# A four-layer pre-norm transformer stack: narrow attention's probabilities and the first attention's queries and keys turned in 64-row halves, ALiBi distances kept once, a value bias carried through the output weights

## The chip, the cores and the metric

The kernel runs on one core of a Trainium2 chip, in fp32 throughout. The metric is the device time of one execution in microseconds; the time given is the median of several runs, and a profile of one execution stands beside it.

## The reference

The input x has 16 sequences of 256 rows of 128 numbers. Four pairs of attention and feed-forward follow, each on the layer norm of x and added to x:

```python
x = x + L0_attn(norm(x))   # 16 heads of 64; queries and keys l2-normalised, scaled; 2 null keys; ALiBi; causal
x = x + L0_ffn(norm(x))    # 128 -> 512 -> gelu -> 128
x = x + L1_attn(norm(x))   # latent of 64; 16 heads of 8, one key and value head for all; causal
x = x + L1_ffn(norm(x))    # gated, then 512 -> 512 -> 512, then 128
x = x + L2_attn(norm(x))   # 16 heads of 64, biases on q, k and v; no mask
x = x + L2_ffn(norm(x))    # 8 experts, the best one for each row
x = x + L3_attn(norm(x))   # 16 heads of 8; window of 128
x = x + L3_ffn(norm(x))    # a gate with the row before
```

In the first attention the score of head h is `8 * (q . k) + dist * slope[h]`, where `dist` is minus the distance of query and key and `slope[h]` falls with h from 0.71 to 1/256. In the third, the value is `xn @ Wv + bv`, and the output `attention @ value @ Wo + bo`.

## The kernel before

The work of each sequence (a batch, b) is cut into steps: `step(engine, rank, ns, emit, r, w, m)` names an engine, a rank (what should come first), an estimate of its length and the tiles that it reads, writes or changes. Nothing is emitted at once. `plan.run()` walks a model of the engines and emits step after step: on each engine the lowest rank among those that could start soon, at most 12 ranks ahead of the first TensorE step that is still open. For TensorE a step also has a `mode`, the shape in which the array is used: "T" for all 128 rows and columns, "S" for two tiles of 64 rows, "O" for two of 64 columns, "S4" and "O4" for four tiles of 32 rows or columns. The plan adds 130 ns where the mode changes. Tiles come from homes with a fixed number of places: eight PSUM banks "t" of 512 columns, three "Q" and three "K", six "pT", six "probs", eight "r", and so on. A step that asks for a place waits until one is free. Each engine carries out its queue strictly in the order that comes out, and waits by semaphores. `evac` copies a PSUM bank into SBUF on ACT or DVE, whichever the plan takes.

Layers are ranked one after the other: 16 batches of the first attention at 16 ranks each, then of the second at 12, and so on; the steps of a batch's preparation lie one batch ahead. Feed-forward steps of two batches follow their attention.

First attention. `prep0` norms and turns x, projects it to queries, keys (`project(n, c)`: n is twice the row block i plus 1 for keys, c the half of the heads) and values. For each raw tile ACT squares, DVE sums over the heads' 64 columns, POOL takes the root (`rsqrt`), DVE multiplies (`scaled`), and TensorE turns four 128x128 blocks into a bank, which goes to Q by `evac`, or to K with the scale of queries and keys (`kqs`) on ACT. Sixteen tables `bias`, one for each head, are made by DVE from the distances `dist`; `first0` adds one to the scores and takes the row minimum of the negated sum. `wide_unit` works on four heads: scores, exponential (`second0`), division on POOL, turned probabilities, products, then `wide_out` through the output weights. It turns its probabilities in two 64-row halves already (line 491):

```python
for z in range(2):
    r, c = slice(64 * z, 64 * z + 64), j * (w // 2) + i * 64
    nc.tensor.transpose(t[z].t[:, c:c + 64], probs[pair].t[r, j, a:a + P], ident[r, r])
```

The halves use the two row tiles of the array at the same time and write into two banks.

Second and last attention. `narrow_unit` has three units to a batch. Four banks of scores (S4), mask and minimum on DVE (line 563), exponentials on ACT, then four turns of four 128x128 blocks each (line 581, mode T), a copy of each bank to "pT", and 16 products of 128 columns in four 32-column tiles (O4). The row sums come out of the products through a column of ones.

Third attention. `prep2` makes queries, keys and values; DVE adds a row `bv`, spread over the partitions by a load, to every values tile (line 1063). `bias_x` adds the output's bias `a2bo` to x on POOL.

Weights. The first load of weights fills `wA`; `to_w1` brings the second layer's into the place that the ALiBi tables held, after the first attention, and `to_w2` the third's into `wA`. These run on SP, as do all large loads.

Lines in the profile: 367 is every product (`mm`), 383 and 385 copies on ACT and DVE, 371 the root on POOL, 431 a turned norm, 474 the division on POOL, 491 and 581 turned probabilities, 744 a small DVE step on the sums, 756 turned queries and keys, 1063 the values' bias.

Of the kernel before, what the change touches and what calls it, by code (L numbers as in the profile page):

```python
# [25 lines left out]
    ("a2bq", 8), ("a2bk", 8),  # L26
# [205 lines left out]
def preln_d4_kernel(ctx: ExitStack, tc: tile.TileContext, x_in, vecs, rows, bv2, nullk, nullv,  # L232
# [50 lines left out]
    bv = cp.tile([P, 1024], F32, tag="bv", name="bv")  # L283
    nc.sync.dma_start(out=bv, in_=bv2.broadcast_to([P, 1024]))
# [74 lines left out]
    plan.home("r", many(sp, "r", 8, [512]))  # L359
# [6 lines left out]
    def mm(o, lhsT, rhs, start=True, stop=True, **kw):  # L366
        nc.tensor.matmul(o, lhsT, rhs, start=start, stop=stop, **kw)  # L367

# [72 lines left out]
    def bias_x(p, name, b):  # L441
        step("POOL", p, 670, lambda e: nc.gpsimd.tensor_tensor(x_of(b), x_of(b), row_over(name, 2), ALU.add), m=[X[b]])  # L442


    def wide_unit(q, b, u, st, widths, starts, blocks, first, second, kept=None):
# [36 lines left out]
        for pair in range(2):  # L482
# [3 lines left out]
            def turn(e, pair=pair, t=t):  # L486
                for j in range(2):
                    for i, a in enumerate(starts):
                        for z in range(2):
                            r, c = slice(64 * z, 64 * z + 64), j * (w // 2) + i * 64  # L490
                            nc.tensor.transpose(t[z].t[:, c:c + 64], probs[pair].t[r, j, a:a + P], ident[r, r])
# [52 lines left out]
    def narrow_unit(q, b, u, st, mask, mkey):  # L544
# [30 lines left out]
        for k in range(4):  # L575
            t, h = get("t"), get("pT")
            pT.append(h)

            def turn(e, k=k, t=t):
                for g in range(4):  # L580
                    nc.tensor.transpose(t.t[:, g * P:(g + 1) * P], probs[g // 2].t[:, g % 2, k * P:(k + 1) * P], ident)  # L581

            step("PE", q + 8 + k, 436, turn, r=probs, w=[t], mode="T")
            evac(q + 8 + k, h, t, lambda h=h, t=t: (h.t, t.t))
# [4 lines left out]
        def products(e):  # L589
# [3 lines left out]
            for k in range(4):  # L593
                hh, kc = (k, 0) if u == 0 else (2 * u - 2 + k // 2, k % 2)
                a = (256 if hh == 3 else 0) + qc * P
                for g in range(4):
                    mm(o.t[32 * g:32 * g + 32, a:a + P], st["v"](kc, g, hh), pT[k].t[:, g * P:(g + 1) * P],
                       u == 0 and k == 0, u == 2 and k == 3, skip_group_check=True)

        step("PE", q + 11.9, 900, products, r=[st["V"]] + pT, m=[o], mode="O4")  # L600
# [50 lines left out]
    bias_pool = top.enter_context(tc.tile_pool(name="a0c", bufs=1))  # L651
# [8 lines left out]
    A0, A1 = 0, first[1, 0]  # L660
    wqkv = wA[:, w0_at["qkv"]:w0_at["qkv"] + 3072]
# [825 lines left out]
```

## Time and profile before

| | us |
|---|---|
| median of 3 runs | 2208.14 |
| lowest and highest | 2207.95, 2212.46 |
| profiled execution, its own time | 2214.85 |
| its span, first to last instruction | 2213.1 |

The mean granted TensorE clock of the profiled execution is 0.990 of full speed. Its DMA engines move 57.78 MB, most of it in the first 60 us and around the loads of weights. The first TensorE instruction starts at 19.45 us, when its weights have landed. The stretches by layer: the first attention to about 640 us, the second with its feed-forward to about 1172, the third to about 1840, where the experts begin to overlap with the last attention (from 1849), and a last stretch of that attention alone from about 2040.

How to read it: a line of the timeline has start, length, engine, line, operation, output and inputs, then rows*columns of the array tile and the shape. A product is two records, since each fp32 product is made in two passes; a turn is one. Lengths of TensorE records overlap[...], so rates are read from starts.

### The profile page before, as it was taken

How to read it: one execution, taken by the hardware profiler on the slowest of the kernel's cores; microseconds unless marked ns; L12 is line 12 of the kernel's file. 1: busy time of each engine (PE TensorE's matmuls, PEld its weight loads, DVE VectorE, ACT ScalarE, POOL GpSimd, SP SyncE). 2: the span in 40 equal slices, each digit the busy share in tenths (PEclk: the TensorE clock that was granted, in tenths of full speed). 3: DMA queues.
4: the chain of work that ended last, by engine and by line, in shares of the span. 5: the costliest groups of instructions: out<-in, count | busy, mean ns of one | idle time of the engine just before them, and what ended most of it. 6: DMA issues, size and time to landing. Idle time of an engine off the chain costs nothing.

```text
span 2213.1 us, 57690 instructions
## 1 busy us (share of the span) xinstructions
PE 2141.7 (97%) x20879; PEld 1576.0 (71%) x20879; DVE 1657.2 (75%) x6401; ACT 1669.9 (75%) x4735; POOL 1054.0 (48%) x1987
## 2 busy tenths in 40 slices
PE   6999999999999999999999999999999999998997
PEld 3767777777776566665666678888888787786775
DVE  5898888889788575666655557877766788787995
ACT  5988888989889776677756567776666577777995
POOL 6997787878851111111103235554543855226331
PEclk9999999999999999999999999999999999999998
DMA  7000000000020000000000000000432000451000
GB/s 173 2 2 2 2 2 2 2 2 2 2 92 2 1 2 1 1 1 1 1 1 1 1 1 7 7 6 3 120 111 82 26 5 19 133 164 28 12 12 11
DMA packets 58590, 57.78 MB, mean 26 GB/s; under 512 B 27824, under 2 KB 48832, under 8 KB 58304
## 3 DMA queue, kind: packets, MB, share of 16 engines
q1 hardware_dynamic: 55504, 49.06, 7.9%
q0 software_dynamic: 2048, 4.20, 0.6%
q8 instruction: 165, 2.70, 0.5%
q14 instruction: 121, 0.99, 0.1%
q10 hardware_dynamic: 752, 0.83, 0.1%
HBM read 43.85 MB, written 10.22 MB: 24 GB/s over the span
## 4 chain that ended last, share of the span: by engine, by line
PE 78%; DVE 10%; POOL 6%; ACT 3%; issue 2%; DMA 1%; another core or an unknown queue 0%; SPq 0%; POOLq 0%; ACTq 0%; DVEq 0%
PE t5x L367 9%; PE t4x L367 8%; PE t7x L367 8%; PE t2x L367 8%; PE t3x L367 7%; PE t0x L367 7%; PE t1x L367 7%; PE t6x L367 7%; PE t0x L581 1%; PE t1x L581 1%; PE t2x L581 1%; PE t3x L581 1%; PE t5x L581 1%; PE t4x L581 1%; PE t6x L581 1%
## 5 line engine op out<-in xcount | busy, mean ns | idle before, releaser
L442 POOL TENSOR_TENSOR x<-x,row_sb 128x256 f32<-128x256 f32 x48 | 35.0, 728 | 31.9 <-DVE xn1x L411 16.0
L404 POOL TENSOR_SCALAR ln_rs1x<-ln_mv1x 128x2 f32<-128x2 f32 x24 | 4.6, 193 | 76.3 <-DVE ln_mv1x L400 73.4
L991 POOL TENSOR_TENSOR x<-x,sq1x 128x512 f32<-128x512 f32 x4 | 5.1, 1280 | 73.2 <-DVE sq1x L989 73.2
L474 POOL TENSOR_SCALAR probs4x<-probs4x,sums6x 128x256 f32<-128x256 f32 (+2 forms) x40 | 17.6, 457 | 38.5 <-DVE sums6x L469 16.9
L474 POOL TENSOR_SCALAR probs2x<-probs2x,sums6x 128x256 f32<-128x256 f32 (+2 forms) x40 | 17.6, 458 | 37.4 <-DVE sums6x L469 21.5
L474 POOL TENSOR_SCALAR probs2x<-probs2x,sums2x 128x256 f32<-128x256 f32 (+2 forms) x44 | 22.2, 519 | 25.8 <-DVE sums2x L469 25.5
L404 POOL TENSOR_SCALAR ln_rs0x<-ln_mv0x 128x2 f32<-128x2 f32 x21 | 4.0, 193 | 63.2 <-DVE ln_mv0x L400 60.2
L371 POOL TENSOR_TENSOR ss0x<-ss0x,mhalf 128x16 f32<-128x16 f32 x11 | 31.9, 2902 | 2.7 <-DVE ss0x L744 2.6
L371 POOL TENSOR_TENSOR ss2x<-ss2x,mhalf 128x16 f32<-128x16 f32 x11 | 32.3, 2934 | 1.6 <-DVE ss2x L744 1.3
L404 POOL TENSOR_SCALAR ln_rs3x<-ln_mv3x 128x2 f32<-128x2 f32 x22 | 4.2, 193 | 58.2 <-DVE ln_mv3x L400 53.2
L371 POOL TENSOR_TENSOR ss1x<-ss1x,mhalf 128x16 f32<-128x16 f32 x11 | 31.9, 2898 | 0.2 <-DVE sums3x L469 0.2
L371 POOL TENSOR_TENSOR ss3x<-ss3x,mhalf 128x16 f32<-128x16 f32 x11 | 31.9, 2896 | 0.0
L474 POOL TENSOR_SCALAR probs4x<-probs4x,sums4x 128x256 f32<-128x256 f32 (+2 forms) x44 | 21.3, 499 | 21.8 <-DVE sums4x L469 21.4
L371 POOL TENSOR_TENSOR ss4x<-ss4x,mhalf 128x16 f32<-128x16 f32 x10 | 29.4, 2942 | 4.7 <-DVE ss4x L744 2.9
L404 POOL TENSOR_SCALAR ln_rs4x<-ln_mv4x 128x2 f32<-128x2 f32 x23 | 4.4, 193 | 57.1 <-DVE ln_mv4x L400 53.8
L474 POOL TENSOR_SCALAR probs4x<-probs4x,sums2x 128x256 f32<-128x256 f32 (+2 forms) x44 | 23.2, 541 | 17.1 <-DVE sums2x L469 9.3
L474 POOL TENSOR_SCALAR probs2x<-probs2x,sums0x 128x256 f32<-128x256 f32 (+2 forms) x44 | 19.4, 459 | 23.8 <-DVE sums0x L469 21.9
L371 POOL TENSOR_TENSOR ss5x<-ss5x,mhalf 128x16 f32<-128x16 f32 x10 | 29.0, 2898 | 0.0
L474 POOL TENSOR_SCALAR probs2x<-probs2x,sums4x 128x256 f32<-128x256 f32 (+2 forms) x44 | 22.1, 515 | 14.1 <-DVE sums4x L469 10.0
L991 POOL TENSOR_TENSOR x<-x,sq0x 128x512 f32<-128x512 f32 x4 | 5.1, 1280 | 45.2 <-DVE sq0x L989 45.2
L474 POOL TENSOR_SCALAR probs5x<-probs5x,sums3x 128x256 f32<-128x256 f32 (+2 forms) x44 | 20.9, 487 | 12.1 <-DVE sums3x L469 9.7
L383 ACT COPY pT1x<-t6x 128x512 f32<-128x512 f32 (+1 forms) x20 | 11.2, 560 | 19.0 <-issue 15.0
(4444 smaller groups left out, 10293.3 us busy)
## 6 DMA issues: line engine op xcount, KB each, us to landing
w0x<-in_wex_dram SPq DMA_DIRECT2D x16, 578.0 KB, 4.0
w1x<-in_wex_dram SPq DMA_DIRECT2D x15, 578.0 KB, 4.0
w2x<-in_wex_dram SPq DMA_DIRECT2D x15, 578.0 KB, 4.0
w_wA<-in_wa_dram SPq DMA_DIRECT2D x8, 512.0 KB, 6.4
ex_rows<-zero SPq DMA_DIRECT2D x2, 1472.0 KB, 23.0
x<-in_x_dram SPq DMA_DIRECT2D x8, 256.0 KB, 7.5
w_wB<-in_wb_dram SPq DMA_DIRECT2D x4, 512.0 KB, 8.0
ex_y<-bT2x SPq DMA_DIRECT2D x17, 64.0 KB, 3.4
```

The lines of the kernel that those rows point to most:

```text
L367: nc.tensor.matmul(o, lhsT, rhs, start=start, stop=stop, **kw)
L371: nc.gpsimd.tensor_tensor(t, t, mhalf[:t.shape[0]].broadcast_to([t.shape[0], n]), ALU.pow)
L383: nc.scalar.copy(o, i)
L404: nc.gpsimd.tensor_scalar(ln.t[2], ln.t[1][:, :, 1], LN_EPS, 1.0, ALU.add, ALU.mult)
L442: step("POOL", p, 670, lambda e: nc.gpsimd.tensor_tensor(x_of(b), x_of(b), row_over(name, 2), ALU.add), m=[X[b]])
L474: nc.gpsimd.tensor_scalar(pr.t[:, j, a:z], pr.t[:, j, a:z], sums.t[:, i:i + 1], 1.0, ALU.mult, ALU.mult)
L581: nc.tensor.transpose(t.t[:, g * P:(g + 1) * P], probs[g // 2].t[:, g % 2, k * P:(k + 1) * P], ident)
L991: step("POOL", lo + 30, 1300, lambda e: nc.gpsimd.tensor_tensor(x, x, ys.t.rearrange("p (c d) -> p c d", d=D), ALU.add), r=[ys, "w1"], m=xx)
```

## The change

Five edits are made together.

1. A helper `turned_halves` turns a 128x128 block in two 64-row halves, into two banks. `narrow_unit` uses it: two turns of eight blocks in mode S in place of four turns of four blocks in mode T. Its products become 32 of 64 columns. `scaled` uses it for queries and keys: one turn takes both row blocks (i = 0 and 1) of one half of the heads, so it waits for both, and the copies go to places of 64 columns.
2. `bias` and its sixteen DVE operations go. The scores are kept divided by the head's slope: the keys' inverse norms are multiplied by 1/slope (`steep`, one small DVE step per row block), null keys likewise (`steepT`), and `first0` adds `dist` and multiplies by minus the slope.
3. The second layer's weights get a place of their own, and `to_w1` moves from rank A1 + 8 (264) to rank 8. `to_w2` moves from rank 326 to 302.
4. The values' bias of the third attention is no longer added to the values. Rows of probabilities sum to one, so it reaches the output as `bv @ Wo`: one step (`through`) makes it on DVE, a product with ones sums it, and it is added to `a2bo` once. Values are copied by `evac`, on either engine, and the load of `bv` goes.
5. The order of the pieces in `prep0` is another, and there are nine "r" places in place of eight. The lead of 26 ranks leaves the spacing as it was, since batches are 16 ranks apart.

```diff
-    bv = cp.tile([P, 1024], F32, tag="bv", name="bv")
-    nc.sync.dma_start(out=bv, in_=bv2.broadcast_to([P, 1024]))
...
+    def turned_halves(t, c, block):
+        for z in range(2):
+            r = slice(64 * z, 64 * z + 64)
+            nc.tensor.transpose(t[z].t[:, c:c + 64], block[r], ident[r, r])
...
-        for k in range(4):
-            t, h = get("t"), get("pT")
+        for kk in range(2):
+            t, h = [get("t"), get("t")], [get("pT"), get("pT")]
             pT.append(h)
-            def turn(e, k=k, t=t):
-                for g in range(4):
-                    nc.tensor.transpose(t.t[:, g * P:(g + 1) * P], probs[g // 2].t[:, g % 2, k * P:(k + 1) * P], ident)
-            step("PE", q + 8 + k, 436, turn, r=probs, w=[t], mode="T")
+            def turn(e, kk=kk, t=t):
+                for k in range(2):
+                    for g in range(4):
+                        turned_halves(t, 256 * k + 64 * g, probs[g // 2].t[:, g % 2, (2 * kk + k) * P:(2 * kk + k + 1) * P])
+            step("PE", q + 8 + 2 * kk, 500, turn, r=probs, w=t, mode="S")
...
-                for g in range(4):
-                    mm(o.t[32 * g:32 * g + 32, a:a + P], st["v"](kc, g, hh), pT[k].t[:, g * P:(g + 1) * P],
-                       u == 0 and k == 0, u == 2 and k == 3, skip_group_check=True)
+                for z in range(2):
+                    for g in range(4):
+                        c = 256 * (k % 2) + 64 * g
+                        mm(o.t[32 * g:32 * g + 32, a + 64 * z:a + 64 * z + 64], st["v"](kc, g, hh), pT[k // 2][z].t[:, c:c + 64],
+                           u == 0 and k == 0 and z == 0, u == 2 and k == 3, skip_group_check=True)
...
-    for u in range(4):
-        step("DVE", 4 * u - 6, 1000, lambda e, u=u: biases(e, u), w=[f"bias{u}"])
+    steep = cp.tile([P, NH], F32, tag="steep", name="steep")
+    for h in range(NH):
+        nc.gpsimd.memset(steep[:, h:h + 1], 1.0 / slopes[h])
...
-        order = ("x p00 p01 p10 p11 p20 p21 t00 p30 t01 p31 t10 v0 t11 v1 v2 t20 v3 t21 t30 t31").split()
+        order = ("x p00 p01 p20 p21 p10 p11 p30 t00 p31 t01 v0 v1 t10 v2 v3 t11").split()
...
+                if which == 1:
+                    step("DVE", p - 6, 80, lambda e: nc.vector.tensor_tensor(ss[n].t, ss[n].t, steep, ALU.mult), m=[ss[n]])
...
-            step("PE", p, 436, turn, r=[raw], w=[t], mode="T")
+            def turn(e):
+                for i in range(2):
+                    for k in range(4):
+                        turned_halves(t, i * 256 + k * 64, of[i].t[:, k * P:(k + 1) * P])
+            step("PE", p, 500, turn, r=of, w=t, mode="S")
...
-                nc.vector.tensor_tensor_reduce(pr.t[:, j, a:z], bank.t[:, a:z], bias[:, 4 * u + k, 258 - (z - a):258],
-                                               -1.0, 3.0e38, ALU.add, ALU.min, nm.t[:, qc:qc + 1])
+                nc.vector.tensor_tensor_reduce(pr.t[:, j, a:z], bank.t[:, a:z], dist[:, 258 - (z - a):258],
+                                               -slopes[4 * u + k], 3.0e38, ALU.add, ALU.min, nm.t[:, qc:qc + 1])
...
-    step("SP", A1 + 8, 2000, to_w1, m=[f"bias{u}" for u in range(4)] + ["w1"], tail=20000)
+    step("SP", 8, 2000, to_w1, m=["w1"], tail=20000)
...
-    step("SP", A1 + 70, 1000, to_w2, m=["wA"], w=["w2"], tail=15000)
+    step("SP", first[0, B - 1] + 62, 1000, to_w2, m=["wA"], w=["w2"], tail=15000)
...
+    step("DVE", first[2, 0] - 12, 1800, through, r=["w2"], w=[bvo])
+    step("PE", first[2, 0] - 8, 224, lambda e: mm(bps.t[:, 0:D], ones, bvo.t[:, 0:D]), r=[bvo], w=[bps], mode="T")
+    step("DVE", first[2, 0] - 8, 200, lambda e: nc.vector.tensor_tensor(row("a2bo"), bps.t[:, 0:D], row("a2bo"), ALU.add), r=[bps], w=["a2bo"])
...
-                step("DVE", p - 8, 600, lambda e, c=c, ps=ps, V=V: nc.vector.tensor_tensor(
-                    V.t[:, c * 512:(c + 1) * 512], ps.t, bv[:, c * 512:(c + 1) * 512], ALU.add), r=[ps], w=[V])
+                evac(p, V, ps, lambda c=c, ps=ps, V=V: (V.t[:, c * 512:(c + 1) * 512], ps.t))
```

## The prediction

> **What bounds the kernel now.** I read the page first: the busy shares, then the forty slices, then the chain that ended last.
>
> ```profile
> PE 2141.7 (97%) x20879; PEld 1576.0 (71%) x20879; DVE 1657.2 (75%) x6401; ACT 1669.9 (75%) x4735; POOL 1054.0 (48%) x1987
> ...
> PE   6999999999999999999999999999999999998997
> ...
> DVE  5898888889788575666655557877766788787995
> ACT  5988888989889776677756567776666577777995
> ...
> PE 78%; DVE 10%; POOL 6%; ACT 3%; issue 2%; DMA 1%; another core or an unknown queue 0%; SPq 0%; POOLq 0%; ACTq 0%; DVEq 0%
> ```
>
> TensorE is busy in nearly every slice and holds 78% of the chain. But near the end (slices 37 and 38) DVE and ACT stand at 9 as well, so one answer for the whole kernel would mislead. So next the busy times by stretch: first attention, second (latent) attention with its feed-forward, third attention, the mixed stretch of experts and last attention, and the last attention alone.
>
> ```profile
> core 0: us, PE busy (x) PEld busy (x) DVE busy (x) ACT busy (x) POOL busy (x), PEclk, DMA share, GB/s
> 60.00:600.00 540.00, 534.90 (x5629) 397.39 (x5626) 464.63 (x1712) 479.57 (x1455) 445.78 (x829) 1.00 0.01 2
> 660.00:1120.00 460.00, 459.78 (x3423) 285.74 (x3420) 306.30 (x1426) 335.22 (x756) 60.37 (x79) 1.00 0.01 1
> 1240.00:1700.00 460.00, 453.40 (x4852) 373.98 (x4848) 320.05 (x866) 310.12 (x1020) 214.61 (x449) 1.00 0.14 40
> 1840.00:2040.00 200.00, 188.73 (x2013) 152.28 (x2017) 161.29 (x837) 155.26 (x417) 76.05 (x129) 0.97 0.32 94
> 2040.00:2190.00 150.00, 145.88 (x1680) 106.08 (x1670) 143.15 (x741) 140.29 (x365) 53.33 (x92) 1.00 0.04 11
> ```
>
> In the second row TensorE never rests and the others have a quarter or more to spare: work taken from it there shortens the kernel. In the first row ACT (480 of 540) and DVE (465) have about a tenth. In the last row DVE has 143 and ACT 140 of 150: they are the bound there as much as TensorE. Last, the timeline of TensorE, for the price of one turned block. Starts are what count: the durations overlap.
>
> ```profile
> 692.16 0.38 PE L581 MATMUL t2x<-ident,probs3x 128*128 128x128 f32 x2
> 692.38 0.38 PE L581 MATMUL t7x<-ident,probs2x 128*128 128x128 f32 x2
> 692.60 0.38 PE L581 MATMUL t7x<-ident,probs3x 128*128 128x128 f32 x2
> 692.91 0.42 PE L367 MATMUL t3x<-pT4x,q1x 128*32 128x128 f32 x8
> 693.16 0.40 PE L367 MATMUL t3x<-pT5x,q1x 128*32 128x128 f32 x8
> 693.37 0.40 PE L367 MATMUL t3x<-pT0x,q1x 128*32 128x128 f32 x8
> ```
> ```profile
> 641.68 0.27 PE L491 MATMUL t1x<-ident,probs5x 64*128 64x64 f32 x1
> 641.68 0.27 PE L491 MATMUL t4x<-ident,probs5x 64*128 64x64 f32 x1
> 641.79 0.22 PE L491 MATMUL t1x<-ident,probs5x 64*128 64x64 f32 x1
> 641.80 0.22 PE L491 MATMUL t4x<-ident,probs5x 64*128 64x64 f32 x1
> 641.85 0.22 PE L491 MATMUL t1x<-ident,probs5x 64*128 64x64 f32 x1
> ...
> 642.58 0.48 PE L367 MATMUL t7x<-xnT0x,wl 128*128 128x256 f32 x1
> ```
>
> A whole block: two in 0.22 us, so 109 ns each. A block in two 64-row halves (two records into two banks): 62 ns. Twelve of them from 641.68 to 642.58 took 0.90 us where 12 x 62 is 0.74: the other 0.16 is the longer first step (0.11) and a gap of 0.10 before the next shape. A change of shape costs such a gap (at 692.60 too: two blocks end their turn at 692.82, the next starts at 692.91) and 0.03 to 0.06 for the first step. I take 0.13 us per change.
>
> **The change part by part.**
>
> Turned blocks. L581 has 1536 records (16 batches x 3 units x 16 blocks x 2 attentions), L756 has 512. All 2048 become halves: 2048 x (109 - 62) ns = -96 us.
>
> Products of the narrow attentions. 96 steps, each 8 groups of four 32-column records at 109 ns (eight records in 0.216 us above), become 16 groups of 64 columns. The nearest row, the wide attention's products at 64 columns, moves from one group to the next in 58 ns: 0.93 for 0.87 us, over 96 steps +5 us. Here a rule speaks against the change. The Trainium skill, "TensorE: Matmul & The Clock Gate", section "Back-to-back issue gap", gives a floor of about 25 ns from start to start, however few columns. A step will have 64 records: 64 x 25 = 1.6 us, so +70 us in all, and the gain would be gone. The records of one group above start about 7 ns apart (the trace shows it for four column tiles and for four row tiles), so a group of four needs 28 ns to issue and lies under its 58. I take +5 and keep +70 as the far end: no row has such a rate sustained.
>
> Changes of shape. The order in which the built program's TensorE instructions stand has 982 changes against 786, because turns of 64-row shape now stand among 128-row work: +31 in the first attention, +77 in the second, 0 in the third, +88 in the last. 196 x 0.13 = +25 us.
>
> TensorE's sum: -96 + 5 + 25 = -66 us. What of it shortens the span goes by stage:
> - First attention: 512 blocks, -24, changes +4: -20. ACT and DVE have a tenth free on average but are full in single slices, and the turns now come late (below). I take 0.7 of it: -14.
> - Second attention: 768 blocks, -36, changes +10, products +2.5: -23. Everything else has room: all of it.
> - Third attention: nothing turned otherwise. The values' bias: 64 adds on DVE of 0.68 us (L1063) go, and 64 copies that ACT (0.59) or DVE may do come. TensorE rests only 6.6 of 460 us there: -2. The bias through the weights is one step of eight small DVE operations, one 128x128 product (0.22 us) and one add, twelve ranks ahead of its use, while DVE is 70% busy: 0; without that cover some 3 us once. POOL's bias add waits for it; behind it stand POOL's divisions.
> - Last attention: -36 + 11 + 2.5 = -22 on TensorE. In 2040:2190 DVE and ACT bind and their work is unchanged: 0. About half of the blocks lie before 2040, where TensorE waits in part for experts: -4. Another rule, "TensorEngine Tiling (Array Packing)", section "PSUM Bottleneck", says that tiling speeds the engine but not the evacuation of its banks. Applied to all stages it makes the whole sum nil; the rows say that it holds in this stage alone (335 and 306 of 460 in the second attention).
>
> Edits at nothing:
> - ALiBi tables: 16 DVE operations of 0.28 us go, 12 of them before TensorE's first instruction at 19.45, which waits for weights. 32 tiny memsets (94 ns each at most, 3 us) go onto POOL's queue ahead of the first layer norm; xn0 was ready at 8.6 us, so 11 us cover them. 32 multiplications of 16 columns (0.17 each by L744, 5 us) join DVE between the roots and the scaling; DVE has 75 us free there.
> - Second weights: the load's seven DMAs move on SP's queue from about 600 us to just behind the zero fills (they end issuing at 36 us), past nothing that waits; SP's next work is far off. The old place cost nothing either (TensorE 20.00 of 20 us in 620:640). The third attention's load moves up by 24 ranks and is used much later: 0. One broadcast load of 512 KB goes: 0.
> - Copies of queries and keys keep their number and size; runs of 64 instead of 128 elements: +-1 us.
>
> Sum: -14 - 23 - 2 - 4 = -43. The profiled execution took 2214.9 us (span 2213.1), 6.7 above the median 2208.1 of the runs; -43 leads to 2172 in its terms, 2165 against the median.
>
> **The rivals.**
>
> All of TensorE's saving arrives, the last attention included, because its evacuations fill gaps that TensorE's own queue makes: -20 - 23 - 2 - 22 = -67, 2141. For it: TensorE is busy 146 of 150 there and leads the chain. Against: DVE at 95%.
>
> PSUM turns short. A narrow turn now takes two of eight banks at once, with scores taking four and each feed-forward step two. If half of the second attention's saving and all but the second's go to waiting, -12: 2196.
>
> Slower: the first attention's scores wait for their keys. Each turn now needs both row blocks of a batch, so the keys' turn moves to the end: in the built order, counted with the durations that the steps carry in the code, the first scores of a batch follow it after 0.9 to 3.8 us of TensorE work, where the last turn of those keys stood 4 to 10 us ahead in most batches. Two key copies on ACT (0.68 each) and one handover must fit in between, on an engine 89% busy. TensorE takes its queue in order, so every microsecond is lost. Sixteen batches: a mean wait of 43 / 16 = 2.7 us each cancels the gain; 4 us each gives +21, 2229. Against: the copies need only 1.5 us when ACT is free.
>
> The change doesn't do what it says: no; the built order has the 4096 half records and no whole ones of these lines.
>
> **How the numbers follow.** The main case (2150 to 2186) 0.52; all saved (2128 to 2150) 0.22; PSUM (2186 to 2204) 0.10; no difference that a measurement could tell, within 0.2% or 4.4 us, 0.04; slower, by late keys or by issue-bound products (far end +70 - 48 = +22), 0.12. Faster: 0.52 + 0.22 + 0.10 = 0.84. Forecast 2165. The range takes the main case, most of "all saved" and most of the PSUM case: 2130 to 2203, with about 0.04 below and 0.15 above.
>
> **What would show it.** Right: TensorE's turns of these lines at 62 ns a block, products near 0.93 us a step, the stretch of the second attention shorter by 20 to 25 us, the last attention alone (DVE and ACT at 95%) as long as before. Wrong: products at over 1.2 us a step; TensorE waiting on K tiles at each batch's first scores; granted clock below 1.00 in the first 1700 us; or the last attention shortened by 15 us or more, which would say that DVE and ACT were not its bound.

## The result, and the profile after

| | us |
|---|---|
| before, median beside the changed kernel | 2208.11 (2207.95 to 2212.46) |
| after, median of 4 | 2192.33 (2191.37 to 2194.72) |
| ratio | 0.9925, interval 0.9908 to 0.9943 |
| span of the profiled executions, before and after | 2213.1, 2190.5 |

The change saves 15.8 us, 0.7%. The forecast was 43: right in sign, inside the range, and nearly three times too large. The chips on which the experiments ran take 2208 to 2215 us for the kernel before, so times are compared within a group that ran on one chip.

First the page's busy times and two rows of slices, after the change (lines of the changed kernel: 365 is every product, 372 a half turn, 388 and 390 copies on ACT and DVE, 767 the scaling of queries and keys, 783 a copy of keys, 927 the add that finishes the second attention's values):

```profile
PE 2097.8 (96%) x26001; PEld 1519.2 (69%) x26001; DVE 1633.5 (75%) x6363; ACT 1695.0 (77%) x4798; POOL 1049.6 (48%) x2019
...
DVE  5898898889888666556655456767665788887996
ACT  4898889889889877678667667777766677777995
```

TensorE's busy time fell by 44 us (from 2141.7), the span by much less than the turned blocks alone should give, and VectorE and ScalarE are within about 25 us of where they were. Next the busy times of the same stretches as before (columns as there):

```profile
core 0: us, PE busy (x) PEld busy (x) DVE busy (x) ACT busy (x) POOL busy (x), PEclk, DMA share, GB/s
60.00:600.00 540.00, 532.03 (x6190) 386.26 (x6190) 480.12 (x1774) 479.15 (x1464) 451.26 (x847) 0.99 0.01 4
660.00:1120.00 460.00, 452.79 (x5381) 267.42 (x5380) 298.93 (x1396) 347.33 (x776) 57.60 (x77) 1.00 0.01 2
1840.00:2040.00 200.00, 182.87 (x3030) 141.06 (x3030) 168.12 (x830) 149.91 (x404) 74.89 (x125) 0.94 0.32 96
```

Three things are new. In the second attention TensorE now rests 7.2 of 460 us where it rested 0.2. In the mixed stretch of experts and last attention it rests 17 of 200 us where it rested 11, and its granted clock is 0.94 in place of 0.97. And the first row has 0.99: the clock falls to half for 6.8 us at 68 us. The timeline of TensorE shows what a half turn looks like where its banks are not both free:

```profile
760.11 0.71 PE L365 MATMUL t5x<-wl,small4x 128*128 128x128 f32 x4
760.75 0.27 PE L372 MATMUL t3x<-ident,probs0x 64*128 64x64 f32 x1
761.44 0.27 PE L372 MATMUL t5x<-ident,probs0x 64*128 64x64 f32 x1 [0.41 <-DVE q1x L927]
761.44 0.27 PE L372 MATMUL t3x<-ident,probs0x 64*128 64x64 f32 x1
761.55 0.22 PE L372 MATMUL t5x<-ident,probs0x 64*128 64x64 f32 x1
761.61 0.22 PE L372 MATMUL t5x<-ident,probs1x 64*128 64x64 f32 x1
...
764.01 0.29 PE L365 MATMUL t1x<-pT3x,q4x 128*32 128x64 f32 x8
764.13 0.29 PE L365 MATMUL t1x<-pT2x,q4x 128*32 128x64 f32 x8
```

The first half goes to bank t3 at 760.75. Its partner must go to t5, which VectorE is still reading (the add that makes the values, line 927), and starts 0.69 us later; the queue stands meanwhile. From then on a pair takes 0.06 us, as forecast (761.55 to 761.61). Two groups of four product records take 0.12 us (764.01 to 764.13): 58 ns a group, as forecast. The waits of TensorE in the second attention, 660 to 1120 us (columns: output, line, released by, us in total, times, longest); before, the same view has no line at all:

```profile
PE t2x L365 <- DVE small4x L390: 0.7, 1, 0.7
PE t4x L372 <- DVE pT2x L390: 0.7, 1, 0.7
...
PE t5x L372 <- DVE q1x L927: 0.4, 1, 0.4
...
```

All lines of the view sum to 6.8 us; the half turns (L372) behind a copy or an add make up 4.7. So where no engine but TensorE was near its limit, the change made waits.

### The profile page after: what moved, and what is told of

It reads as the page before. It is cut to its first block, busy times and chain, and to the rows that moved or that the text cites. A ratio compares the mean times of both kernels' runs of the same rounds, so it can differ in the third digit from the quotient of the medians.

```text
span 2190.5 us, 68042 instructions
## 1 busy us (share of the span) xinstructions
PE 2097.8 (96%) x26001; PEld 1519.2 (69%) x26001; DVE 1633.5 (75%) x6363; ACT 1695.0 (77%) x4798; POOL 1049.6 (48%) x2019
## 5 line engine op out<-in xcount | busy, mean ns | idle before, releaser
L479 POOL TENSOR_SCALAR probs0x<-probs0x,sums6x 128x256 f32<-128x256 f32 (+2 forms) x44 | 19.2, 453 | 25.8 <-DVE sums6x L474 18.7
L479 POOL TENSOR_SCALAR probs4x<-probs4x,sums6x 128x256 f32<-128x256 f32 (+2 forms) x40 | 17.6, 454 | 27.2 <-DVE sums6x L474 19.9
L479 POOL TENSOR_SCALAR probs0x<-probs0x,sums2x 128x256 f32<-128x256 f32 (+2 forms) x40 | 18.6, 478 | 24.4 <-DVE sums2x L474 24.3
L479 POOL TENSOR_SCALAR probs2x<-probs2x,sums4x 128x256 f32<-128x256 f32 (+2 forms) x40 | 19.2, 491 | 22.5 <-DVE sums4x L474 22.1
```

The source lines that it names most:

```text
L479: nc.gpsimd.tensor_scalar(pr.t[:, j, a:z], pr.t[:, j, a:z], sums.t[:, i:i + 1], 1.0, ALU.mult, ALU.mult)
```

## The stretches that are compared

A stretch's end is read from the start of a TensorE record in the timeline: the first product with the null values (`nv_out`) of batch 1 and of batch 14 (batches count from 0), the last product with the second layer's weights (`w_wB`), the last scores of the third and of the last attention. "TensorE time" is the sum over the stretch's records of the start-to-start time that their form has where nothing interrupts it (whole turn 109 ns, pair of halves 62, group of 64-column products 58, a pass of 512 columns 430). What a stretch takes beyond that is changes of shape and waits. The ends of the second row, in the kernel before (run again) and after (of the two products with `w_wB` the last record starts 0.11 us behind the first):

```profile
629.59 0.37 PE L367 MATMUL t7x<-nv_out,small4x 32*128 32x128 f32 x1
1311.62 0.39 PE L367 MATMUL t0x<-w_wB,r7x 128*128 128x128 f32 x2
```
```profile
618.80 0.37 PE L365 MATMUL t1x<-nv_out,small4x 32*128 32x128 f32 x1
1293.10 0.39 PE L365 MATMUL t4x<-w_wB,r5x 128*128 128x128 f32 x2
```

| us | before, run again | other edits alone | after | forecast of the change |
|---|---|---|---|---|
| start to batch 1 | 125.6 | 131.1 | 128.4 | |
| first attention, batch 1 to 14 | 504.0 | 498.1 | 490.4 | -14, with the row above |
| to the second layer's last product | 682.1 | 685.4 | 674.4 | -23 |
| third attention | 516.7 | 516.7 | 516.0 | -2 |
| experts and last attention | 341.3 | 340.5 | 343.9 | -4 |
| to the end | 37.6 | 37.5 | 37.3 | |
| span | 2207.3 | 2209.3 | 2190.5 | -43 |

("Before, run again" and "other edits alone" are the last and the first experiment of the next section.) The second and third row repeat within 0.5 us from run to run of one program in nearly all runs. The first row does not: kernels that begin alike, with whole or halved turns later on, took 127.4 to 131.0 us for it. The rows of the experts and the last attention differ by several us between chips.

## Experiments: the parts by themselves

One group, in which the kernel before took 2209.35.

**Other edits alone.** Both uses of the halves undone, and the pieces of `prep0` in their old order, which goes with whole turns; everything else of the change stays.

```diff
-        order = ("x p00 p01 p20 p21 p10 p11 p30 t00 p31 t01 v0 v1 t10 v2 v3 t11").split()
+        order = ("x p00 p01 p10 p11 p20 p21 t00 p30 t01 p31 t10 v0 t11 v1 v2 t20 v3 t21 t30 t31").split()
...
-            step("PE", q + 8 + 2 * kk, 500, turn, r=probs, w=t, mode="S")
+            step("PE", q + 8 + k, 436, turn, r=probs, w=[t], mode="T")
...
-            step("PE", p, 500, turn, r=of, w=t, mode="S")
+            step("PE", p, 436, turn, r=[raw], w=[t], mode="T")
```

> The changed kernel with whole 128x128 turns everywhere (queries, keys and narrow probabilities as before); the ALiBi, weights and values' bias edits stay. Theory (the saving of the halves is real but about 0.17 us per change of array shape and waits for the second PSUM bank take most of it back): these edits alone are worth 0 to -4 us, 2204 to 2208. Rival (the other edits cost time and hide a larger gain of the halves): 2212 or more.

Measured 2212.14, ratio 1.0016 (1.0006 to 1.0025): ALiBi, loads, values' bias and the ninth "r" place cost 2.8 us together: the rival's case.

**Queries and keys in halves, narrow turns whole** (of the edits above, only that of the narrow turns).

> The changed kernel with the narrow probabilities turned whole again; halves for first attention's queries and keys only. Theory: the first attention gains about 1 us a batch less 3 us at the start, so 2195 to 2200, and the narrow halves are worth only 3 to 8 us in the changed kernel. Rival (the narrow halves carry the gain as forecast, about 20 us): 2210 or more.

Measured 2200.63, ratio 0.9961 (0.9948 to 0.9973), at the upper end of what was expected: 11.5 us below the other edits alone. The new order of `prep0` is in this too; it was not tried alone.

**Narrow turns in halves, queries and keys whole, in their old order** (the other two edits above).

> The changed kernel with first attention's queries and keys turned whole and in the old order; narrow halves stay. Theory: 2196 to 2202 (the second attention's 6 to 12 us remain), and the granted clock does not fall near 68 us, if the late first turns cause that fall. Rival (queries and keys in halves are worth nothing because ACT and DVE bind the first attention): 2190 to 2194, as the changed kernel.

Measured 2203.22, ratio 0.9977 (0.9968 to 0.9987): 8.9 below the other edits alone, and 1 us above the theory's range. The parts add: 2.8 - 11.5 - 8.9 = -17.6 beside -15.8. The clock falls near 70 us here as well (6.8 us), and for 3.4 us with the other edits alone, but not in the kernel before: the late half turns don't cause that fall.

**The kernel before again.**

> The kernel before, unchanged, to see its profile at the median time. Theory: 2208, and the 6.7 us by which the first profiled execution stood above the median lie in a stretch where the granted clock fell. Rival: they are spread over the span.

Measured 2208.64, ratio 0.9999 (0.9989 to 1.0008). Its span, 2207.3, is 5.8 below that of the profile that the forecast was read from; to 1311 us the two are alike, and the difference lies behind that. Behind 1700 us its clock stands at half speed for 34.6 us, and for 44.3 in the other: at half speed those 9.7 us make up at most 4.9 of the 5.8, so the expectation can hold for most of it; that was not shown.

So the narrow halves, three quarters of the halved blocks, bring the smaller part. With whole or halved turns (other edits alone, and after) the accounts are:

| stretch | TensorE time | shape changes | rest of the stretch |
|---|---|---|---|
| first attention, batch 1 to 14 | 452.6 to 434.2 | 239 to 268 | 45.5 to 56.2 |
| to the second layer's last product | 638.4 to 604.9 | 189 to 271 | 47.0 to 69.5 |

TensorE's own time falls as forecast, by 18.4 us for 13 of 16 batches and by 33.5 us with the products' share in it. But each added change comes with 0.37 us in the first (10.7 over 29, the new order's effect included) and 0.27 in the second (22.5 over 82), not 0.13. The next question is whether that is a change's price or waits. Listed waits of TensorE grow from nothing to 3.7 us in the first of these rows and from 1.9 to 9.5 in the second.

## Experiments: the price of a change of shape

The group's kernel before took 2214.35.

**An extra block ahead of each narrow turn** of the second attention:

```diff
             def turn(e, kk=kk, t=t):
                 for k in range(2):
+                    if k == 0 and mkey == "mask1":
+                        nc.tensor.transpose(t[0].t[:, 0:128], probs[0].t[:, 0, 2 * kk * P:(2 * kk + 1) * P], ident)
                     for g in range(4):
```

> The changed kernel with one more transpose of a full 128x128 block ahead of each of the second attention's 96 narrow turns, into a bank that the turn overwrites: the output is the same, and TensorE gets 96 blocks of 109 ns (10.5 us) and 98 shape changes more (1080 against 982 in its order). Theory A (a change costs 0.17 us of TensorE's own time, and TensorE binds there): +10.5 and +16.7, so 27 us above the changed kernel, within 5. Theory B (0.13 as forecast): +23. Theory C (in the second attention TensorE waits for others and extra TensorE work is absorbed): under 12.

**The same block in the middle of the turn:**

```diff
+                    if k == 1 and mkey == "mask1":
+                        nc.tensor.transpose(t[0].t[:, 256:384], probs[0].t[:, 0, 2 * kk * P:(2 * kk + 1) * P], ident)
```

> The same extra blocks, but each in the middle of its turn, between the two groups of eight 64-row pairs: the same instructions as the kernel with the block ahead, in the same order otherwise, with 94 shape changes more (1174 against 1080). The difference of the two kernels is the price of 94 changes alone. Theory A: 0.17 us each, 16 us slower than with the block ahead. Theory B: 0.13 each, 12 us. Theory C (a change costs only where a wait follows): under 5 us.

Measured 2221.01 (ratio 1.0028) and 2235.66 (1.0095): 14.65 us for 94 changes, 0.156 each; in the stretch itself, 693.4 and 708.2, 0.157. That lies between theory A's 0.17 and theory B's 0.13, nearer to A, and it is not free of waits: those listed in this stretch sum to 5.0 us with the block ahead and 7.3 in the middle. Without these 2.3 us a change would be at 0.13. The timeline of the kernel with the block in the middle shows what the price is made of:

```profile
702.75 0.22 PE L372 MATMUL t3x<-ident,probs1x 64*128 64x64 f32 x1
702.91 0.33 PE L585 MATMUL t3x<-ident,probs0x 128*128 128x128 f32 x1
703.17 0.27 PE L372 MATMUL t3x<-ident,probs0x 64*128 64x64 f32 x1
703.28 0.23 PE L372 MATMUL t3x<-ident,probs0x 64*128 64x64 f32 x1
...
703.56 1.13 PE L365 MATMUL t1x<-xnT0x,w_wB 128*128 128x512 f32 x2
704.52 1.02 PE L365 MATMUL t0x<-xnT0x,w_wB 128*128 128x512 f32 x2
```

Of each pair the first record is shown. The last pair would end its turn at 702.81; the whole block starts at 702.91, 0.10 later. The whole block takes 0.26 to the next start, 0.15 more than its 0.109: its own longer step, and the gap before the halves. The first pair takes 0.11, 0.05 more than later ones. Together 0.30 for two changes, 0.15 each; the 96 blocks of the run have a median of 0.30 as well. Behind the turn comes a product of 512 columns: its two records take 0.96 us where two take 0.86 in a row (2 x 0.43), so a way back that ends in a product costs 0.05 more than one that ends in a turned block.

The block ahead of the turn is as telling. By 0.156 a change it should add 96 x 0.109 + 98 x 0.156 = 25.8 us to the stretch; it adds 693.4 - 674.4 = 19.0, less than either theory had. Its waits over 660 to 1120 us sum to 2.4 us in place of 6.8, and the ones behind the add are 0.3 in place of 0.4. The extra work lies in part where TensorE had been waiting. So of the second attention's 22.5 us, 82 x 0.156 = 12.8 are the price, and some 10 are waits and idle starts, of which the extra blocks covered about 7. This split is an estimate: with 0.13 to 0.17 for a change it is 11 to 14 and 9 to 12, and the listed waits grew by 7.6.

**The planner charged 300 ns for a change in place of 130:**

```diff
-    WINDOW, STAY, TURN, SWITCH = 12.0, 4.0, 3.0, 130
+    WINDOW, STAY, TURN, SWITCH = 12.0, 4.0, 3.0, 300
```

> The changed kernel with one number of the planner changed: a step that would change TensorE's shape is charged 300 ns instead of 130, so that the planner groups steps of one shape. Shape changes in TensorE's order fall from 920 steps' worth to 846. Theory A (a change costs some 0.17 us of TensorE where TensorE binds, and the changes ate the gain): 5 to 12 us faster, 2180 to 2187 us. Theory B (a change costs little, or what is saved is lost to later operands because steps now wait for their group): within 3 us of 2192, or slower.

Measured 2224.29, ratio 1.0038 (1.0024 to 1.0052), in a group whose kernel before took 2215.05: slower than both kernels. 74 changes fewer, and every stretch from batch 1 on is longer than in the changed kernel's order on the same chip: 683.7 for 674.4 to the second layer's last product, 521.5 for 517.5 in the third attention, where no turn was changed. Theory A's gain did not come. This doesn't speak against the price, which the pair above measures: in the second row 17 changes went and the rest of the stretch still grew by 8 us, with listed waits of 14.2 in place of 9.5. Grouped by shape, steps wait for each other more.

**Are the waits for a second bank the missing part?** The add of line 927 is given a longer time in the planner (on a kernel with halves in the second attention only, see below), so that no turn is put right behind it:

```diff
-        step("DVE", lo, 330, lambda e: nc.vector.tensor_tensor(V.t.rearrange(
+        step("DVE", lo, 700, lambda e: nc.vector.tensor_tensor(V.t.rearrange(
```

> Halves in the second attention only; and the planner's length of the values' add in that attention is 700 ns instead of 330, so that no turn is placed right behind the products whose bank the add still reads. TensorE's shape changes are 890 against 894 without. Theory A (the wait for a turn's second bank costs 0.7 us a time there): the stretch from the 14th batch's end to the last use of the second layer's weights, 674.5 us in every run of the changed kernel so far, falls by 4 to 8 us, and the waits behind the add are gone from TensorE's list. Theory B (the wait only moves to the next operand): the stretch stays within 2 us of 674.5.

**The same for every handover:**

```diff
-    TAIL = {"PE": 165, "ACT": 110, "DVE": 95, "POOL": 30, "SP": 0}
+    TAIL = {"PE": 165, "ACT": 250, "DVE": 300, "POOL": 30, "SP": 0}
```

> Halves in the second attention only; and the planner counts 300 and 250 ns instead of 95 and 110 between the end of a VectorE or ScalarE step and its users, everywhere, so that turns are placed behind banks that are surely free. 893 shape changes. Theory A: the second attention's stretch falls by 5 to 10 us from 674.5; elsewhere the order changes too, with an effect of either sign. Theory B: the stretch stays or grows, since TensorE takes other steps first and operands come later, as when 300 ns was charged for a change of shape (+18 us in this stretch).

Measured 2198.38 and 2197.99 beside 2214.10 (both 0.9931, 0.9915 to 0.9948). The stretch is 677.0 and 677.5, longer than 674.5, and by a little more than theory B's 2 us. (The expectation names +18 us for the planner's 300 ns in this stretch; it is +9.) Theory A falls, for this remedy. In the first kernel five waits behind the add became one, in the second none is left, and others took their place: all listed waits of 660 to 1120 us sum to 6.4 and 8.5 us, where the kernel without the remedy has 6.8.

```profile
PE t6x L372 <- DVE pT2x L390: 0.7, 1, 0.7
PE t2x L372 <- ACT pT2x L388: 0.6, 1, 0.6
...
PE t5x L372 <- DVE q1x L949: 0.4, 1, 0.4
```

So the waits don't hang on one late bank: when one is taken out of the way, another is not yet free. Whether a layout with fewer banks to a turn would end them was not tried.

## Experiments: the last attention

**Halves in the second attention only**, whole turns in the last:

```diff
-            narrow_unit(first[3, b] + 4 * u, b, u, st, mask3, "mask3")
+            narrow_unit(first[3, b] + 4 * u, b, u, st, mask3, "mask3", False)
```

(`False` picks the whole turns and 128-column products of the kernel before.)

> Narrow probabilities turned in halves in the second attention only; the last attention turns them whole, as before. Theory A (the last attention is bound by VectorE and ScalarE, which are 97 to 99% busy there, so TensorE time saved in it is given back): within 2 us of the changed kernel's 2192, and the stretch from the end of the third layer to the end of the span stays at 379 to 381 us. Theory B (TensorE time counts there as in my sum, half of -33 us of nominal time at least): the stretch grows and the kernel takes 2197 to 2209 us. Theory C (the extra shape changes make halves a loss there): 2186 to 2190 us.

**A later rank for the second weights' load:**

```diff
-    step("SP", 8, 2000, to_w1, m=["w1"], tail=20000)
+    step("SP", 70, 2000, to_w1, m=["w1"], tail=20000)
```

> The changed kernel with the load of the second layer's weights moved from rank 8 (the start) to rank 70 (the middle of the first attention, some 200 us in). Theory A (the early load takes DMA time from the start and delays it by the +5.5 us seen from the first scores to the first batch's end): about 5 us faster, 2186 to 2189 us, and the clock's fall at 68 us is gone. Theory B (the start is later because queries and keys are turned from two projections at once, or because of the new order of projections and the ALiBi edits): 2191 to 2194 us, with the fall still there.

This one moved nothing: SyncE has nothing to wait for, runs ahead and still loads at once, and the order on the four compute engines is the changed kernel's. So neither theory was tested, and the run counts as the changed kernel on that chip: 2200.69, and the kernel with whole turns in the last attention 2192.71 (ratios 0.9933, 0.9916 to 0.9949, and 0.9900, 0.9883 to 0.9917). The halves there cost 8.0 us: theory C of the first of the two. (The expectation's own 2192 and 379 to 381 us are those of another chip; 2192.71 and 380.6 us look like theory A only until they are set beside the changed kernel's 2200.69 and 388.1 on this one.) With the planner's 300 ns in both the pair says the same:

> Both: whole turns in the last attention and 300 ns for a shape change in the planner; 768 shape changes. If the last attention gains nothing from halves and changes cost 0.17 us each: 2180 to 2187 us, at or below the kernel with 300 ns alone. If halves in the last attention do save TensorE time that counts: 5 us or more above the kernel with 300 ns alone.

Measured 2217.51 beside 2224.29: 6.8 us faster with whole turns. The level that was expected (2180 to 2187) was missed, as for the kernel with 300 ns alone. The forecast's reason for no gain there was that VectorE and ScalarE bind. Two kernels relieve them, one with whole turns and one with halves in the last attention:

```diff
+        ncp = 128 if mkey == "mask3" else 512
...
-                evac(q + 8 + k, h, t, lambda h=h, t=t: (h.t, t.t))
+                evac(q + 8 + k, h, t, lambda h=h, t=t: (h.t[:, 0:ncp], t.t[:, 0:ncp]), n=ncp)
```

The copies of half turns are cut in the same way. Both kernels leave out three quarters of each of these copies, so they serve for their times alone.

> Halves in the second attention only; and in the last attention the copies of turned probabilities out of PSUM move 128 of 512 columns, so the last attention works on stale probabilities in the other columns: some 96 copies of VectorE and ScalarE take about 0.4 us less each, 38 us less work for the two engines together over the stage. Theory A (those two bind the last attention): 8 to 19 us faster than the kernel with full copies (2192 us). Theory B (TensorE binds it): no faster.

> The same with the last attention's turns in halves too. Without the relief the halves there gained nothing (they were 8 us slower on one chip). Theory A (they gain nothing because VectorE and ScalarE bind, and TensorE's waits bring its clock down): with those two relieved the halves' 33 us of saved TensorE time counts at least in part, 5 to 20 us below the relieved kernel with whole turns. Theory B (shape changes and waits for second banks ate the gain, whatever the other engines do): equal to the relieved kernel with whole turns within 3 us, or slower.

Measured 2184.41 and 2192.11 (ratios 0.9867 and 0.9899). In experts and last attention the relief brings 7.6 us with whole turns and 6.4 with halves (335.7 for 343.3 and 343.1 for 349.5). These two differences are taken across two chips, whose kernels before are within 0.7 us of each other, so that those engines bind in part is likely and not shown. On one chip, the halves lose 7.7 us with the relief, as they lost 8.0 without it on the other. Theory A falls. (VectorE stays at 95 and 98% in 2040 to 2140 us, so the relief wasn't whole.) The size of the loss depends on the chip: in the first group the stretch takes 340.9 us with narrow halves (queries and keys whole), and 340.5 and 343.0 in the two kernels with whole turns, so there the halves cost nothing that could be told.

What costs the time, where it is lost? The accounts suggested the clock: with halves in the last attention it stands at half speed for 34 to 55 us between 1700 and 2100 us in every kernel up to here, with whole turns for 17 to 27. So TensorE was given the time back without a change of shape:

```diff
                     for g in range(4):
-                        turned_halves(t, 256 * k + 64 * g, ...)
+                        for again in range(2 if mkey == "mask3" and g < 3 else 1):
+                            turned_halves(t, 256 * k + 64 * g, ...)
```

> The changed kernel with three of every four pairs of half turns in the last attention done twice, to the same place: the output and the order of shapes stay, and TensorE gets some 576 pairs of 62 ns more (36 us), which is the time that whole turns would take. Theory A (with halves TensorE waits so often in the last attention that its clock is halved for longer, and so the saved time comes back): the clock's falls between 1700 and 2100 us shrink from about 37 to 41 us to about 20, and the time is within 5 us of the changed kernel run beside it, or below it. Theory B (shape changes and second banks eat the gain): all of it lies on TensorE's path, 15 to 36 us slower.

Beside it ran the changed kernel,

> The changed kernel again, beside the others on their chip: 0.9925 of the kernel before, with its clock at half speed for 35 to 41 us between 1700 and 2100 us.

and the version with whole turns there (its load held back as well, see below):

> Halves in the second attention only, whole turns in the last, and the load of the second layer's weights held back as in the run before. If the load matters, 2 to 5 us below the kernel with second-attention halves alone, which was 0.990 of the kernel before: 0.988; if it doesn't, 0.990. Either way faster than the changed kernel beside it, by 5 us or more if the last attention's halves are a loss on every chip.

Measured, beside 2208.28 for the kernel before: filled halves 2210.30 (1.0007), changed kernel 2194.01 (0.9932, 0.9915 to 0.9948), whole turns in the last attention 2189.67 (0.9910, 0.9894 to 0.9927), 4.3 us below the changed kernel where 5 or more was expected. The busy times of 1840 to 2040 us, for the changed kernel, the filled one and the one with whole turns, in this order (columns as above):

```profile
1840.00:2040.00 200.00, 182.90 (x3030) 141.09 (x3030) 168.05 (x831) 149.91 (x404) 74.85 (x125) 0.94 0.32 96
```
```profile
1840.00:2040.00 200.00, 187.65 (x3521) 152.63 (x3509) 164.51 (x800) 144.83 (x390) 73.25 (x123) 0.97 0.33 95
```
```profile
1840.00:2040.00 200.00, 189.78 (x1995) 151.80 (x1992) 170.00 (x874) 156.06 (x420) 77.58 (x128) 0.97 0.33 96
```

The filler brings the clock back to 0.97, and the kernel is 16 us slower for it. Theory A, that the clock takes the gain, falls too: the lower clock goes with TensorE's rests. It may still have a share: 37.5 us at half speed against 23.9 with whole turns cost at most (37.5 - 23.9) / 2 = 6.8 us. The accounts of experts and last attention (third attention's last scores to the last attention's) say more:

| | TensorE time | shape changes | stretch |
|---|---|---|---|
| whole turns | 271.0 | 156 | 340.1 |
| halves, filled up to the same time | 271.2 | 238 | 356.8 |
| halves | 237.8 | 238 | 343.9 |

From the first to the second row TensorE's time is the same, and shapes, banks and the number of records differ: 82 more changes come with 16.7 us, 0.20 each. From the second to the third 33.4 us of TensorE time go and 12.9 come off the stretch: 39% gets through, the rest goes in waits and the lower clock. 16.7 - 12.9 = +3.8 us: the halves are a loss on this chip. How the 16.7 splits into price (82 x 0.156 = 12.8 by the second attention's figure) and waits for banks was not measured apart.

## Experiment: the start

**The second weights' load held back in earnest,** behind a write of GpSimd into its place:

```diff
+    step("POOL", 60, 100, lambda e: nc.gpsimd.memset(w1["t"][:, 0:1], 0.0), m=["w1"])
+    step("SP", 62, 2000, to_w1, m=["w1"], tail=20000)
```

> The changed kernel with the load of the second layer's weights made to wait: GpSimd writes one column of their buffer at rank 60 (some 300 to 450 us in), and SyncE's load comes behind that. Theory A (the load at 35 to 60 us crowds the start): the first batch's end comes 2 to 5 us earlier, the clock's fall at 68 us is gone or shorter, and the time is 2 to 5 us below the changed kernel run beside it. Theory B (the start's order of projections, not the load): the start and the time are the same within 1.5 us.

The timeline of its DMA queue shows that it now waits:

```profile
145.25 3.73 SPq L264 DMA_DIRECT2D w_wB<-in_wb_dram  x7
```

Measured 2192.66 (2191.19 to 2193.92) beside 2194.01 (2192.11 to 2194.45) for the changed kernel: 1.3 us, with overlapping runs. Batch 1's end comes 0.9 us earlier, and the clock's fall at the start is 3.4 us long in place of 6.8. In the kernel with whole turns in the last attention, its load held back too, that fall is 6.8 us long and batch 1's end comes at 130.9 us. So nothing here shows that the load makes the start late: theory B in that. Theory B's own cause, the order of projections, isn't it either: with the other edits alone, in the old order and with whole turns, batch 1 ends 5.5 us later than before. By batch 14 the two stand level (629.2 and 629.6 us), but by the sum of start-to-start times TensorE has then done about 2 us less of its work, so part of the later start is lost.

## Why the prediction was wrong, step by step

- **Turned blocks, -96:** right. Pairs take 62 ns, and TensorE's own time fell by 18.4 (13 batches), 33.5 and 33.2 us in the three stretches, products included.
- **Products, +5, with the rule on the issue gap as far end** (the Trainium skill, "TensorE: Matmul & The Clock Gate", section "Back-to-back issue gap")**:** right. A group takes 58 ns; a floor of 25 ns from start to start would be 100 for its four records, and the second attention could not have become shorter. The rule did not hold for these records of different column tiles.
- **Changes of shape, 196 x 0.13 = +25, and waits for banks at nothing: this is the step that failed.** The count was right (982 against 786). Alone, a change costs 0.15 by its rows, not far from 0.13; I had priced the gap and the first pair of halves, and left out that a way back into a product has a first step that is longer by 0.10 us. The larger part of the error is waits, which the sum had at nothing: a half turn needs two free banks, or two finished tiles, and TensorE's queue stands until it has them. Price and waits together measured 0.37 each in the first attention (forecast +4, measured 10.7 for 13 batches, the new order included), 0.27 in the second (forecast +10, measured 22.5) and 0.20 in the last (forecast +11, measured 16.7): 10.7 + 22.5 + 16.7 = 50 us, twice what the sum had.
- **First attention, -14:** the halves brought -7.7 from batch 1 to 14 and -11.5 in the whole kernel. The factor 0.7 was meant for late keys and full engines; changes and waits took more. The slower rival's wait, scores behind a copy of keys, is in the profile once, for 0.5 us; a half turn that waits for the scaling of its second tile, 0.8 us once, is the longest:

```profile
PE t5x L372 <- DVE r7x L767: 0.8, 1, 0.8
...
PE t3x L365 <- ACT K2x L783: 0.5, 1, 0.5
```

- **Second attention, -23, all of it:** -11.0 against the other edits alone, and -7.7 against before. This is the PSUM rival, which I gave one chance in ten: half turns wait for their second bank. It named half of the saving as lost, and half is what was lost: by the estimate above 82 x 0.156 - 10 = 2.8 us to the price of changes, the other 9 or so to waits. I had counted a stage in which everything else has room as free of waits.
- **Third attention, -2:** -0.7, and 0.0 with the other edits alone, in which the adds are gone as well. TensorE binds, and adds on VectorE were hidden.
- **Last attention, -4:** +2.6 against the kernel before run again, -0.5 against the profile that the forecast was read from; halves against whole turns, each pair on one chip, +0.4, +3.8, +6.3 and, with the relief, +7.5. I counted the changes of shape as free there with the saved time. They are not: where it was measured, TensorE's saved time counts at 39%, and shapes and banks cost 16.7.
- **Edits at nothing:** +2.8 together. No run shows the load as the cause; which of the others is, stays open. The granted clock did fall below 1.00 in the first 1700 us, the sign that I had named, but it falls without the halves too.
- The rule of the Trainium skill, "TensorEngine Tiling (Array Packing)", section "PSUM Bottleneck", that tiling doesn't speed the emptying of banks, I let speak for the last attention only. In the second attention half turns wait behind copies of banks as well, with DVE busy 299 and ACT 347 of 460 us: not a full engine, as the rule has it, but a single bank that comes late.

The best version that was run is the changed kernel with whole turns in the last attention: 8.0 us below the changed order in one group, 4.3 in another (there with the load held back, and without overlap: 2188.25 to 2191.52 against 2192.11 to 2194.45).

## What to carry to other kernels

A faster form of one instruction is bought with its entries and exits: count the changes of shape by stage and price one from a row that goes in and comes back (here 0.30 us for the pair). A form that takes two banks at once waits for the later of the two (0.69 us in the place shown); waits that a profile of the old form does not have can't be read from it, so they belong in the sum with a bound. Where other engines are nearly full, what is saved counted in part here (39%), while the added changes and waits cost 16.7 us: weigh the two stage by stage.

## What was not expected of the hardware

- A whole block between two half turns takes 0.26 us to the next start, against 0.109 in a row of its kind. The gap is the same both ways (0.09 to 0.10 us); the first step is longer by 0.05 us into halves, and by 0.10 into a product on the full array.
- The granted clock goes to half for 3.4 to 20.5 us at a time where TensorE's rests become frequent: 37.5 us in all between 1700 and 2100 us with halves in the last attention, 23.9 with whole turns on the same chip. Extra work shortened this to 27.3 and did not pay.
- A load without anything to wait for ran as soon as its queue reached it, whatever its rank: at 35 us with rank 8 and with rank 70 alike, at 145 us once it had a wait.
